# Layer 0 of a four-layer convolution kernel: q (kᵀ v) of two heads as one product with the masked pair, in place of two products on halves of the array

## The chip, the cores and the metric

The kernel runs on one core of one Trainium2 chip. The metric is the device time of the whole program in microseconds (us), the median of three runs. Where a profile is quoted, it is of one execution of the program, with its own time.

## The reference, cut to what matters

x has the shape (T=4, B=8, N=512, D=512). Four layers are added to it one after the other, each on a normalised x. The change lies in layer 0, a spiking attention without softmax; layer 1 is a 13x13 convolution per channel, layers 2 and 3 are 3x3 convolutions over the channels, layer 2 with quantised values.

```python
T, B, N, D, H = (4, 8, 512, 512, 8)
DH = D // H                                   # 64
scale = 1.0 / np.sqrt(D).astype(np.float32)
q = heads(lif(bn(x @ Wq.T, ...)))             # heads: (T, B, H, N, DH), spikes 0 or 1
k = heads(lif(bn(x @ Wk.T, ...)))
v = heads(lif(bn(x @ Wv.T, ...)))
scores = jnp.einsum('tbhnd,tbhmd->tbhnm', q, k) * scale
bias = bias_table[rel].transpose(2, 0, 1)     # depends on m - n and the head alone
scores = scores + bias[None, None]
out = jnp.einsum('tbhnm,tbhmd->tbhnd', scores, v)
out = lif(out.transpose(0, 1, 3, 2, 4).reshape(T, B, N, D))
out = lif(bn((out * gate_scale + gate_shift) @ Wp.T, ...))
```

As there is no softmax, (q kᵀ) v is computed as q (kᵀ v): kᵀ v is only 64x64 for each head. The bias part is a Toeplitz matrix times v, added to it.

## The kernel before

**Steps.** Layer 0 goes through 32 steps (b, t). A step has two halves in the program: `attend` of this step, and then the projections of the next step's input to v, k and q (`project_in`, L499, f32, whole array) with the output projections of this step (`project_out`, L562) between them. So on TensorE's queue a step reads: L515, then L535 with L527 among them, then L499 with L562 among them. The tiles' scheduler sets the order within each engine's queue by priority and readiness as it builds the program[...].

**`attend`, by lines.**

- L515: kᵀ v. The 512 columns of D are four pairs of heads, j = 0 to 3, each 128 columns wide. For each j four products of 128x128 add up a 128x128 block in `ps_kv`: on its diagonal kᵀ v of the two heads, 64x64 each; off the diagonal the products of one head's k with the other head's v, which nobody needs.
- L520: VectorE multiplies all four blocks with a mask of ones in the two diagonal 64x64 squares and zeros elsewhere, and writes them as f16 to `kvb`.
- L527: for each j and each head `two` of the pair, the 128 rows and 64 columns of `kvb` that belong to the head are the stationary operand, and q of the pair (128 rows, 512 columns) streams past. The result lands in 64 partitions of `ps_a`. The first head uses columns 0 to 63 of the array and the second columns 64 to 127 (the trace writes this as 128*64).
- L535: the bias part. For each j 24 products of the same form: 4 blocks of v, 3 bf16 parts of the Toeplitz matrix (`toep`), 2 heads. They add up in `ps_b`, also on 64-column halves.
- L545 (ScalarE, t = 0) or L547 (VectorE) reads `ps_a`; L550 (VectorE) adds `ps_b`; `fire` (L444 and what follows) makes the spikes `so` of this j, which L562 reads.

`ps_a` has one buffer, `ps_b` two, `ps_kv` one. Because `kvb` comes from VectorE, the scheduler puts some L535 between L515 and the first L527 of a step (8, 16 or 9, as it comes), and after that 24 L535 between one pair of L527 and the next.

**After layer 0.** Layer 1 (L815) starts on TensorE when the last step's output projection is done; it uses 112*64 of the array. Layers 2 (L1098, 128*128, bf16) and 3 (L1200, 64*64, f32) run together at the end, a few of one and a few of the other.

Of the kernel before, what the change touches and what calls it, by code (L numbers as in the profile page):

```python
# [45 lines left out]
DH = D // H  # L46
# [220 lines left out]
def layer0(  # L267
    s, tc, i, x_in, x1d, ident, block, avg, group_stats, st1, norm1, band1d, r1, w_sum, shared
):
    nc = tc.nc  # L270
# [171 lines left out]
    def fire(v, h, t, c_col, spikes):  # L442

        nc.vector.tensor_scalar(spikes, v, 1.0, None, op0=ALU.is_ge)  # L444
        if t < T - 1:
            nc.vector.scalar_tensor_tensor(v, v, 1.0, v, op0=ALU.is_lt, op1=ALU.mult)  # L446
            if c_col is None:
                nc.scalar.mul(h, v, 0.5)
            else:
                nc.scalar.activation(h, v, AF.Identity, bias=c_col, scale=0.5)  # L450
# [57 lines left out]
    def attend(got, t):  # L508
        q, k, v = got["q"], got["k"], got["v"]

        kv = ps_1.tile([P, NC, P], F32, tag="misc", name="ps_kv")
        for j in range(NC):
            cut = slice(j * P, (j + 1) * P)
            for c in range(NC):
                nc.tensor.matmul(  # L515
                    kv[:, j, :], lhsT=k[:, c, cut], rhs=v[:, c, cut],
                    start=c == 0, stop=c == NC - 1,
                )
        kvb = work.tile([P, NC, P], F16, tag="kvb", name="kvb")
        nc.vector.tensor_mul(kvb, kv, block.unsqueeze(1).to_broadcast([P, NC, P]))  # L520
        spikes = work.tile([P, NC, N], F32R, tag="so", name="so")
        for j in range(NC):
            pa = ps_1.tile([P, N], F32, tag="pa", name="ps_a")
            pb = ps_b.tile([P, N], F32, tag="pb", name="ps_b")
            for two in range(2):
                out = slice(two * DH, (two + 1) * DH)
                nc.tensor.matmul(  # L527
                    pa[out, :], lhsT=kvb[:, j, out], rhs=q[:, j, :], start=True, stop=True
                )
            for c in range(NC):  # L530
                u = P * (NC - 1 - c)
                for z in range(3):
                    for two in range(2):
                        h = 2 * j + two
                        nc.tensor.matmul(  # L535
                            pb[two * DH : (two + 1) * DH, :],
                            lhsT=v[:, c, h * DH : (h + 1) * DH],
                            rhs=toep[z][:, h, u : u + N],
                            start=c == 0 and z == 0,
                            stop=c == NC - 1 and z == 2,  # L540
                        )
            h = h_of["o"][:, j, :]
            w = work.tile([P, N], F32, tag="v", name="v_o", bufs=3)
            if t == 0:
                nc.scalar.mul(w, pa, half_scale)  # L545
            else:
                nc.vector.scalar_tensor_tensor(  # L547
                    w, pa, half_scale, h, op0=ALU.mult, op1=ALU.add
                )
            nc.vector.scalar_tensor_tensor(w, pb, 0.5, w, op0=ALU.mult, op1=ALU.add)  # L550
            fire(w, h, t, None, spikes[:, j, :])
        return spikes
# [102 lines left out]
    for n in range(-1, last + 1):  # L655
        b, t = steps[max(n, 0)]
        if n >= 0:
            with tc.issue_after(did) if n == 0 else ExitStack():
                so = attend(spikes, t)
            residual = load_x(b, t, "xr")  # L660
            if n == last:
                head = start_layer1()
        if n + 1 <= last:
            spikes = new_spikes()
            g, j = divmod(n + 1, PAIR * T)
# [632 lines left out]
```

## Time and profile before

| | |
|---|---|
| runs | 2936.95, 2939.95, 2939.79 us |
| median of the runs | 2939.79 us |
| the profiled execution | 2938.79 us, span 2937.0 us |
| granted TensorE clock, mean | 0.986 |
| layer 0 on TensorE (first to last of L499 and `attend`) | until about 2050 us |
| layer 1 (L815) | 2050.6 to 2500.9 us |
| layers 2 and 3 (L1098, L1200) | 2513.6 us to the end |
| L535, 3072 matmuls | 368.4 us in which at least one runs, 383 ns each |
| L527, 256 matmuls | 379 ns each (median) |
| L515, 512 matmuls | 219 ns each (median) |

How to read it: [...] the next one starts before it ends. So the time that a matmul takes from the queue is the distance from its start to the start of the next one, called its slot below, and not its duration. The product of the count and the duration says little: 3072 times 383 ns would be three times the 368.4 us in which L535 runs at all. In the listings PE is the matmul, PEld the load of its stationary operand, DVE is VectorE; what stands in brackets is the idle time of the engine before the instruction, and what ended it.

The whole list of costs on the page names L499 first (three rows of some 450 us each), and then L815, L535 and L562; L527 is too small to be among the shown rows.

### The profile page before, as it was taken

How to read it: one execution, taken by the hardware profiler on the slowest of the kernel's cores; microseconds unless marked ns; L12 is line 12 of the kernel's file. 1: busy time of each engine (PE TensorE's matmuls, PEld its weight loads, DVE VectorE, ACT ScalarE, POOL GpSimd, SP SyncE). 2: the span in 40 equal slices, each digit the busy share in tenths (PEclk: the TensorE clock that was granted, in tenths of full speed). 3: DMA queues.
4: the chain of work that ended last, by engine and by line, in shares of the span. 5: the costliest groups of instructions: out<-in, count | busy, mean ns of one | idle time of the engine just before them, and what ended most of it. 6: DMA issues, size and time to landing. Idle time of an engine off the chain costs nothing. (4 is left out here: it accounts for less than half of the span.)

```text
span 2937.0 us, 36614 instructions
## 1 busy us (share of the span) xinstructions
PE 2833.3 (96%) x12865; PEld 1303.7 (44%) x12865; DVE 2214.3 (75%) x3915; ACT 551.2 (19%) x859; POOL 1035.3 (35%) x1928
## 2 busy tenths in 40 slices
PE   6899999999999999999999999999999999589999
PEld 3454555554555545455455555455333333223334
DVE  7897788789779778878877886886655566887870
ACT  1300010011010001001001000110211112766664
POOL 3343234333234323323422433332211112676650
PEclk9899999999999999999999999999999999889999
DMA  7323322222222222222221122113877779698865
GB/s 180 97 81 81 76 58 66 66 73 77 69 61 70 71 75 73 58 66 66 76 68 46 49 54 55 51 42 95 226 194 216 201 208 247 142 204 209 222 171 147
DMA packets 323943, 322.10 MB, mean 110 GB/s; under 512 B 21639, under 2 KB 237391, under 8 KB 323647
## 3 DMA queue, kind: packets, MB, share of 16 engines
q1 hardware_dynamic: 261504, 236.70, 32.9%
q0 software_dynamic: 20192, 56.83, 6.2%
q10 hardware_dynamic: 42063, 26.23, 3.2%
q8 instruction: 101, 1.65, 0.2%
q14 instruction: 83, 0.68, 0.1%
HBM read 210.57 MB, written 103.60 MB: 107 GB/s over the span
## 5 line engine op out<-in xcount | busy, mean ns | idle before, releaser
L499 PE MATMUL ps_in<-w_v,xn 128*128 128x512 f32 x1024 | 459.7, 599 | 3.0 <-DVE xn L480 3.0
L499 PE MATMUL ps_in<-w_kq,xn 128*128 128x512 f32 x1024 | 450.2, 592 | 0.0
L815 PE MATMUL ps_conv<-x,bt 112*64 112x512 f32 x2048 | 445.1, 592 | 0.8 <-DVE v_p L467 0.8
L499 PE MATMUL ps_in<-xn,w_kq 128*128 128x512 f32 x1024 | 444.6, 592 | 0.0
L535 PE MATMUL ps_b<-toep,vtok 128*64 128x512 bf16 x3072 | 368.4, 383 | 1.0 <-DVE v_o L550 1.0
L475 POOL TENSOR_TENSOR h_v<-h_v,c_v 128x512 f32<-128x512 f32 x96 | 121.9, 1270 | 685.1 <-DVE h_v L474 659.4
L450 ACT ACTIVATE h_q<-v_q,c_half 128x512 f32<-128x512 f32 x96 | 69.2, 721 | 1473.0 <-DVE v_q L446 865.1
L584 POOL COPY x1s<-x1s 128x2 f32<-128x2 f32 (+1 forms) x1024 | 227.8, 278 | 272.8 <-DVE x1s L573 272.8
L562 PE MATMUL ps_out<-wp,so 128*128 128x512 f32 x1024 | 308.8, 444 | 0.0
L499 PEld LDWEIGHTS ps_in<-xn,w_kq 128*128 128x128 f32 x1024 | 194.3, 190 | 233.0 <-issue 222.0
L499 PEld LDWEIGHTS ps_in<-w_kq,xn 128*128 128x128 f32 x1024 | 194.2, 190 | 219.9 <-issue 205.0
L499 PEld LDWEIGHTS ps_in<-w_v,xn 128*128 128x128 f32 x1024 | 191.0, 191 | 218.6 <-issue 210.3
L815 PEld LDWEIGHTS ps_conv<-x,bt 112*64 112x64 f32 x2048 | 145.5, 135 | 289.7 <-issue 287.8
L1200 PE MATMUL ps_conv<-x,band_t 64*64 64x512 f32 x2040 | 252.5, 612 | 3.1 <-DVE band_t L1169 3.1
L1065 POOL COPY u<-x 128x512 f32<-128x512 f32 (+1 forms) x172 | 209.3, 1252 | 99.6 <-issue 51.8
L535 PEld LDWEIGHTS <-vtok 128*64 128x64 bf16 x3072 | 175.6, 111 | 154.7 <-issue 5.6
L562 PEld LDWEIGHTS ps_out<-wp,so 128*128 128x128 f32 x1024 | 192.6, 188 | 94.3 <-issue 58.3
L573 DVE SCALAR_TENSOR_TENSOR x1s<-v_p,xr 128x256 f32<-128x256 f32 x256 | 188.6, 776 | 13.9 <-DMA x<-x1s 3.1
L833 POOL DMA_DIRECT2D x<-xo x128 | 71.4, 565 | 313.7 <-ACT xo L822 299.4
L475 POOL TENSOR_TENSOR h_k<-h_k,c_k 128x512 f32<-128x512 f32 x96 | 123.2, 1283 | 135.1 <-DVE h_k L474 135.1
L822 ACT ACTIVATE xo<-ps_conv,off 128x512 f32<-128x512 f32 x128 | 87.9, 687 | 430.9 <-PE ps_conv L815 315.1
L1105 DVE SCALAR_TENSOR_TENSOR x<-ps_conv,inv,u 128x512 f32<-128x512 f32 (+1 forms) x172 | 121.7, 745 | 57.8 <-PE ps_conv L1098 30.6
(190 smaller groups left out, 3279.7 us busy)
## 6 DMA issues: line engine op xcount, KB each, us to landing
x<-x SPq DMA_DIRECT2D x64, 917.0 KB
x<-x SPq DMA_DIRECT2D x168, 256.0 KB
x<-x1s POOLq DMA_DIRECT2D x128, 262.0 KB, 2.6
xq<-in_x SPq DMA_DIRECT2D x128, 256.0 KB
xr<-in_x SPq DMA_DIRECT2D x128, 256.0 KB
out<-o SPq DMA_DIRECT2D x164, 192.0 KB
xs<-in_x SPq DMA_DIRECT2D x112, 256.0 KB
x<-xo ACTq DMA_DIRECT2D x128, 128.0 KB
```

The source lines that it names most:

```text
L475: nc.gpsimd.tensor_add(h, h, c_twice[n])
L499: mm = nc.tensor.matmul(ps, lhsT=lhsT, rhs=rhs, start=k == 0, stop=k == NC - 1)
L535: nc.tensor.matmul(pb[two * DH : (two + 1) * DH, :], lhsT=v[:, c, h * DH : (h + 1) * DH], rhs=toep[z][:, h, u : u + N], start=c == 0 and z ...
L562: nc.tensor.matmul(ps, lhsT=so[:, k, c * P : (c + 1) * P], rhs=wpT[z][:, k, :], start=k == 0 and z == 0, stop=k == NC - 1 and z == 1,)
L573: nc.vector.scalar_tensor_tensor(own, v.rearrange("p (g v) -> p g v", g=PH)[:, two, :], 1.0, by_phase[:, two, :], op0=ALU.is_ge, op1=ALU.add,)
L584: nc.gpsimd.tensor_copy(x1[:, f, u : u + n], x1[:, fm, um - n + 1 : um + 1][:, ::-1])
L815: mm = nc.tensor.matmul(ps[q * M1 : (q + 1) * M1, :], lhsT=bt[:, z, :], rhs=xt[:, w0 : w0 + N_PS1, z : z + NV], start=z == 0, stop=z == SH ...
L822: nc.scalar.activation(xo[:, a, :], ps, AF.Identity, bias=off[:, t : t + 1])
L833: engine.dma_start(bass.AP(dst.tensor, dst.offset + (q * n_half * W1_OUT * B + b) * D + f * NV, [[B * D, W1_OUT], [W1_OUT * B * D, n_half] ...
L1065: nc.gpsimd.tensor_copy(u[:n_p, j, :].rearrange("p (v g) -> p v g", g=PH), x[:, j, :].rearrange("p (g v) -> p v g", g=PH),)
L1105: done["DVE"] = nc.vector.scalar_tensor_tensor(own, ps[:n_p, :], w["inv"][:n_p], u[:n_p, j, :], op0=ALU.mult, op1=ALU.add, accum_out=sums[ ...
L1200: mm = nc.tensor.matmul(ps[j][b * HALF : (b + 1) * HALF, :], lhsT=band[half, b, dx, :], rhs=x3[half, s0 + j, dx : dx + D], start=dx == 0, ...
```

## The change

The inner loop over the two heads of a pair is gone. One matmul has the whole 128x128 block of `kvb` as its stationary operand, and writes all 128 partitions of `ps_a`. As the mask has put zeros into the off-diagonal squares, each head's 64 rows of the result hold the same sums, with zeros added. Nothing else in the program's text changes; the lines below it move up by four, so that L535 becomes L531, and the one product stands at L525.

```diff
         for j in range(NC):
             pa = ps_1.tile([P, N], F32, tag="pa", name="ps_a")
             pb = ps_b.tile([P, N], F32, tag="pb", name="ps_b")
-            for two in range(2):
-                out = slice(two * DH, (two + 1) * DH)
-                nc.tensor.matmul(
-                    pa[out, :], lhsT=kvb[:, j, out], rhs=q[:, j, :], start=True, stop=True
-                )
+            nc.tensor.matmul(pa, lhsT=kvb[:, j, :], rhs=q[:, j, :], start=True, stop=True)
             for c in range(NC):
                 u = P * (NC - 1 - c)
                 for z in range(3):
```

The order of the changed program on TensorE is that of the program before with one load and one product in each place where two and two stood, apart from two L535 that move in the first step and one L499 in three places. On the other engines the order is the same.

## The prediction

> **What bounds the kernel now.** I read the page's busy times, then the sums of the stretch in which the changed code runs, then the instructions in order of time inside one time step, then the weight loads' waits.
>
> ```profile
> PE 2833.3 (96%) x12865; PEld 1303.7 (44%) x12865; DVE 2214.3 (75%) x3915; ACT 551.2 (19%) x859; POOL 1035.3 (35%) x1928
> ```
> ```profile
> 174.00:2042.00 1868.00, 1857.97 (x7614) 939.28 (x7611) 1498.36 (x2496) 138.12 (x209) 632.22 (x1363) 1.00 0.25 65
> ```
>
> The first is the busy time of each engine over the span; the second the sums over 174 to 2042 us, steps 1 to 31 of layer 0: TensorE (first pair of numbers) has an instruction in flight for 1857.97 of 1868.00 us at a granted clock of 1.00, VectorE (third pair) for 1498.36. So in layer 0 TensorE's queue is the clock: a slot added or removed there moves the end, as long as TensorE doesn't then wait for someone. Busy time can't show how full the slots are; the order in time can:
>
> ```profile
> 1038.48 1.45 PE L499 MATMUL ps_in<-xn,w_kq 128*128 128x512 f32 x3
> ...
> 1039.77 1.06 PE L515 MATMUL ps_kv<-vtok,k 128*128 128x128 bf16 x16
> ...
> 1040.76 1.05 PE L535 MATMUL ps_b<-toep,vtok 128*64 128x512 bf16 x8
> 1041.10 0.68 DVE L520 TENSOR_TENSOR kvb<-ps_kv,c 128x512 f16<-128x512 f32 x1
> 1041.84 0.11 PEld L527 LDWEIGHTS <-kvb 128*64 128x64 f16 x2 [0.51 <-DVE kvb L520]
> 1041.84 0.41 PE L527 MATMUL ps_a<-q,kvb 128*64 128x512 f16 x2
> ...
> 1042.08 1.89 PE L535 MATMUL ps_b<-toep,vtok 128*64 128x512 bf16 x16
> ...
> 1043.59 0.11 PEld L527 LDWEIGHTS <-kvb 128*64 128x64 f16 x2
> 1043.81 0.38 PE L527 MATMUL ps_a<-q,kvb 128*64 128x512 f16 x2
> ...
> 1044.02 2.76 PE L535 MATMUL ps_b<-toep,vtok 128*64 128x512 bf16 x24
> ...
> 1049.63 2.76 PE L535 MATMUL ps_b<-toep,vtok 128*64 128x512 bf16 x24
> ...
> 1052.32 1.13 PE L499 MATMUL ps_in<-w_v,xn 128*128 128x512 f32 x2
> ```
>
> The columns are start, length, then engine, line and the part of the array used (rows*columns). Two things matter. First, the two halves already run side by side: the pair of L527 starts at 1043.81 and the next L535 at 1044.02, and 24 L535 take from 1044.02 to 1046.61 (the next L527 in the same listing): 2.59/12 = 0.216 us a pair, for two products of 512 columns. A pair of halves costs what one product costs. Second, a gap appears wherever the array changes between 64-column halves and the whole array. The last of 16 L515 starts at 1039.77+1.06-0.219 (its duration) = 1040.61, its slot of 0.056 ends at 1040.67, yet L535 starts at 1040.76: 0.093 us of nothing. The last pair of L535 starts at 1049.63+2.76-0.38 = 1052.01, its slot ends at 1052.22, L499 starts at 1052.32: 0.096. Between L499 and L515, both on the whole array though of different types, there is none: the third L499 starts at 1039.34 and its slot of 0.429 ends at 1039.77, where L515 starts.
>
> [...] loads of L515 (128 columns) last 98 ns, of L527 (64 columns) 110 ns, so the whole block's load is no dearer than one half's.
>
> **The change part by part.** It removes 128 of 256 matmuls and loads at L527; the lines below move up by four. [...] DVE's multiplication with the block mask (L520) already makes the off-diagonal blocks zero, so no work is added to prepare it.
>
> *The slot itself.* 0.216 for the pair, 0.216 for one product: nothing gained but the 3 ns between the halves' starts.
>
> *The two changes of mode.* The product now stands alone between column-tiled L535, 24 of them on either side. Layer 2 and 3 hold the same figure, a whole-array 16-bit product between tiled ones:
>
> ```profile
> 2699.79 2.81 PE L1200 MATMUL ps_conv<-x,band_t 64*64 64x512 f32 x24
> 2702.53 1.47 PE L1098 MATMUL ps_conv<-xq,band 128*128 128x512 bf16 x6
> 2703.93 2.81 PE L1200 MATMUL ps_conv<-x,band_t 64*64 64x512 f32 x24
> 2706.67 1.47 PE L1098 MATMUL ps_conv<-xq,band 128*128 128x512 bf16 x6
> ```
>
> From 2702.53 to 2703.93 is 1.40 us for six products, where 6 x 0.216 = 1.30: 0.10 more. Single starts in the trace split it: first product to second 227 ns instead of 216 (its load, 95 ns, isn't ahead of it and is only partly covered: +11), the last to the next L1200 308 = 216 + 92. On the way in, the last group of L1200 to L1098 takes 522 instead of a slot of 429: +93. And the first L535 pair after a change takes 240 ns instead of 216 (L515 to L535, all 32 times): +24.
>
> *A visit in the stream* therefore adds: 96 in, 11 for the load, 93 out, 24 for the next pair's load = 224 ns. Steps 1 to 31 have three each (j = 1 to 3), 93 visits: 20.83 us.
>
> *The first visit of a step* (j = 0) waits for kvb anyway: the last pair before it starts at 1041.43 [...]. The way in is hidden behind that wait; without it 96 ns more. The pair after the wait took 240 ns, the product will take 227: -13, and then 93+24: 104 ns. 31 visits: 3.22 us. In the seven steps where half a pair of L535 stands ahead of the product the wait is 326 ns after that half's start, more than 309, so the same holds; an odd half alone ahead of a change takes a slot, but the staggered order ended in such a half before, too: 47 slots both ways.
>
> *The first step* (92 to 124 us) is mixed with other whole-array work. Visits 3 and 4 stand between L499 there, so the change takes two changes of mode away: each now costs 523-429 = 94 on the way in, 24 in the pair, 96 on the way out and about 104 in the next f32 product: 318 ns, twice, -0.64 us. Visits 1 and 2 have whole-array work before and L535 after: one change either way, nothing.
>
> Sum: 20.83 + 3.22 - 0.64 = +23.4 us. No stall goes: kvb is as late as before, and the L547 that reads ps_a gets it one product later as before. Queued behind each delayed product are L535, then L550 on DVE and the next step's L499: all move by the same amount. Nothing covers it, as TensorE is the longest queue. The profiled execution took 2938.79 us (span 2937.0, 1.8 around it): 2962.2. The median of the runs is 1.0 above it: 2963.2.
>
> **The rivals.** *No price for the change of mode (ends not slower).* The gaps of 0.09 could belong to what stands at those places, a semaphore or another bank, and a 128-column product between 64-column ones may slip in. Place: the 124 visits of steps 1 to 31; price 0; the sum would be 128 x 3 ns = -0.4, and -0.6 from step 0 falls away as well: 2939.4. It decides once a visit costs under 5 ns, the pair's own small cost. Against: L515 to L535 share type and operands (vtok) and still show 0.093, all 32 times within 1 ns, in the same place as L1200 to L1098; L499 to L515 shows none.
>
> *Part is absorbed.* Seven steps after the first wait longer for kvb than the usual 0.3 to 0.5 us, up to 2.7:
>
> ```profile
> PE ps_a L527 <- DVE kvb L520: 8.8, 7, 2.3
> ```
>
> DVE is behind there, at 1220 to 1230 without a pause, after a wait for a load of xs. If that load doesn't move along with TensorE, the 0.776 us that a step adds (3 x 0.224 + 0.104) are absorbed in each: 7 x 0.78 = 5.4, giving 2957.8. Against: DVE's work and the buffers of xs follow TensorE's step.
>
> *The load is dearer.* For f32 the first product after a change has 104 ns more. If a 98 ns load of f16 lay bare wholly, 98-11 = 87 more for 93 visits: 8.1 us, 2971.3. L1098's 227 speaks against it.
>
> **How the numbers follow.** Forecast 0.82, part absorbed 0.06, dearer load 0.07, no price 0.05. The unknown costs from both sides: the load between 0 (-11 x 93 = -1.0 us) and bare (+8.1); step 0 between 0 and -0.64; absorption 0 to 5.4. All these end slower. I take 2957 to 2969, which holds the forecast, the absorbed case and most of the way to the dear load. 0.2%, about what a measurement can tell from no change, is 5.9 us; no case but the first rival is inside it, and a little is left for a gain that I don't see: faster 0.01, same 0.04, slower 0.95.
>
> **What would show it.** In the changed kernel's listing: one L525 between L531, with the load no longer ahead of it but at its own start; L531's last start to L525 0.31, L525 to L531 0.32, the first L531 pair 0.24; the period of one j 3.03 us instead of 2.81; a step 0.78 longer, layer 1 starting 23 us later and as long as before. Wrong would be a period of 2.81 (no price), or longer waits at L499 for xn (DVE as the bound).

## The result, and the profile after

The changed kernel takes 2956.01 us in the median of four runs, the kernel before 2938.37 us in the median of its four (the three runs listed above and one of 2936.52): a ratio of 1.007, with a 95% interval of 1.0058 to 1.0082. It is slower, by 17.6 us between the medians. The profiled execution took 2955.41 us, with a span of 2953.6 us.

The busy times of the page, and the sums over 171 to 2042 us, most of steps 1 to 31 of layer 0 (which now end at 2072), show little (the same columns as before):

```profile
PE 2850.1 (96%) x12737; PEld 1292.5 (44%) x12737; DVE 2218.3 (75%) x3915; ACT 550.7 (19%) x859; POOL 1033.6 (35%) x1928
```
```profile
171.00:2042.00 1871.00, 1862.48 (x7355) 919.77 (x7353) 1488.29 (x2479) 138.11 (x209) 631.07 (x1363) 1.00 0.25 64
```

TensorE has 128 matmuls fewer and is busy for 17 us longer: the gaps at a change of mode (about 0.1 us) don't show as idle time, as in the trace the matmul that started 0.31 us earlier lasts 0.38 us and so is still running. Where the time went is seen in the order of time. This is the same step as was shown of the kernel before (start, length, engine, line, operation):

```profile
1052.22 1.05 PE L531 MATMUL ps_b<-toep,vtok 128*64 128x512 bf16 x8
...
1053.30 0.10 PEld L525 LDWEIGHTS <-kvb 128*128 128x128 f16 x1 [0.51 <-DVE kvb L520]
1053.30 0.39 PE L525 MATMUL ps_a<-q,kvb 128*128 128x512 f16 x1
...
1053.62 1.92 PE L531 MATMUL ps_b<-toep,vtok 128*64 128x512 bf16 x16
...
1055.46 0.10 PEld L525 LDWEIGHTS <-kvb 128*128 128x128 f16 x1 [0.41 <-issue]
1055.47 0.39 PE L525 MATMUL ps_a<-q,kvb 128*128 128x512 f16 x1
...
1055.79 2.78 PE L531 MATMUL ps_b<-toep,vtok 128*64 128x512 bf16 x24
...
1058.50 0.39 PE L525 MATMUL ps_a<-q,kvb 128*128 128x512 f16 x1
```

The load of the pair (L527) used to start 0.22 us ahead of its product (1043.59 against 1043.81); now the load at L525 starts at 1055.46 with the product at 1055.47. The 16 L531 before it end their last slot at 1055.37 (1053.62+1.92-0.38 = 1055.16 for the last start, and a slot of 0.21), and the product starts at 1055.47, so no product starts for 0.10 us although the last one's slot is over. From L525 to the next L531 it takes 0.32 us, of which 0.216 is the product's slot. The period of one j is 1058.50-1055.47 = 3.03 us, 2.81 before. The wait for kvb ahead of the first product is 0.51 us as it was.

Cut at the same places of the trace, the two executions compare like this (us; the middle row runs from the first L515 of step 1 to the first matmul of layer 1):

| | before | changed | difference |
|---|---|---|---|
| start and step 0 | 173.40 | 170.48 | -2.9 |
| steps 1 to 31 of layer 0 | 1877.17 | 1901.94 | +24.8 |
| layer 1, until the first matmul of layer 2 | 463.06 | 463.40 | +0.3 |
| layers 2 and 3 | 423.38 | 417.80 | -5.6 |
| span | 2937.0 | 2953.6 | +16.6 |

So layer 0 lost what was expected of it, and 8.5 us came back at both ends, where the change was to take 0.64 us away in the one (step 0) and nothing in the other. The last row is seen in the order of time of layers 2 and 3. First the kernel before, then the changed one, at the same work:

```profile
2672.76 0.57 PE L180 MATMUL gps_x<-gsum_x,avg_same 128*128 128x1 f32 x2 [2.15 <-DVE gsum_x L177]
2673.26 4.25 PE L1200 MATMUL ps_conv<-x,band_t 64*64 64x512 f32 x24
```
```profile
2694.06 0.38 PE L180 MATMUL gps_x<-gsum_x,avg_same 128*128 128x1 f32 x2 [2.15 <-DVE gsum_x L177]
2694.37 2.81 PE L1196 MATMUL ps_conv<-x,band_t 64*64 64x512 f32 x24
```

TensorE waits 2.15 us for VectorE in both. Behind that wait the 24 matmuls of layer 3 take 4.25 us in the one and 2.81 in the other. The granted clock goes with it: over the last 260 us (window; busy times of PE, PEld, DVE, ACT, POOL; granted clock, DMA share, GB/s) it is 0.97 before and 1.00 in the changed kernel.

```profile
2673.60:2937.00 263.40, 253.18 (x1858) 93.36 (x1850) 152.00 (x268) 163.51 (x259) 126.12 (x177) 0.97 0.71 182
```
```profile
2695.80:2953.60 257.80, 246.16 (x1850) 90.93 (x1842) 155.17 (x266) 162.60 (x259) 124.56 (x177) 1.00 0.72 185
```

Two questions were left: a proof of the mechanism in layer 0, and whether these 8.5 us are the change's.

### The profile page after: what moved, and what is told of

Same layout as the page of the kernel before. It is cut to its first block, busy times and chain, and to the rows that moved or that the text cites. A ratio compares the mean times of both kernels' runs of the same rounds, so it can differ in the third digit from the quotient of the medians.

```text
span 2953.6 us, 36334 instructions
## 1 busy us (share of the span) xinstructions
PE 2850.1 (96%) x12737; PEld 1292.5 (44%) x12737; DVE 2218.3 (75%) x3915; ACT 550.7 (19%) x859; POOL 1033.6 (35%) x1928
## 5 line engine op out<-in xcount | busy, mean ns | idle before, releaser
L499 PE MATMUL ps_in<-w_v,xn 128*128 128x512 f32 x1024 | 459.3, 599 | 3.0 <-DVE xn L480 3.0
L499 PE MATMUL ps_in<-w_kq,xn 128*128 128x512 f32 x1024 | 450.2, 592 | 0.0
L499 PE MATMUL ps_in<-xn,w_kq 128*128 128x512 f32 x1024 | 444.6, 592 | 0.0
L531 PE MATMUL ps_b<-toep,vtok 128*64 128x512 bf16 x3072 | 370.8, 386 | 1.1 <-DVE v_o L546 1.1
L499 PEld LDWEIGHTS ps_in<-xn,w_kq 128*128 128x128 f32 x1024 | 194.3, 190 | 233.0 <-issue 222.0
L499 PEld LDWEIGHTS ps_in<-w_kq,xn 128*128 128x128 f32 x1024 | 194.2, 190 | 219.9 <-issue 205.0
L499 PEld LDWEIGHTS ps_in<-w_v,xn 128*128 128x128 f32 x1024 | 191.0, 191 | 218.6 <-issue 210.3
L1196 PE MATMUL ps_conv<-x,band_t 64*64 64x512 f32 x2040 | 245.1, 596 | 3.1 <-DVE band_t L1165 3.1
L531 PEld LDWEIGHTS <-vtok 128*64 128x64 bf16 x3072 | 162.8, 111 | 163.0 <-issue 34.2
L546 DVE SCALAR_TENSOR_TENSOR v_o<-ps_b,v_o 128x512 f32<-128x512 f32 x128 | 88.4, 691 | 114.7 <-PE ps_b L531 114.7
```

Source lines behind the costliest of these rows:

```text
L499: mm = nc.tensor.matmul(ps, lhsT=lhsT, rhs=rhs, start=k == 0, stop=k == NC - 1)
L531: nc.tensor.matmul(pb[two * DH : (two + 1) * DH, :], lhsT=v[:, c, h * DH : (h + 1) * DH], rhs=toep[z][:, h, u : u + N], start=c == 0 and z ...
L1196: mm = nc.tensor.matmul(ps[j][b * HALF : (b + 1) * HALF, :], lhsT=band[half, b, dx, :], rhs=x3[half, s0 + j, dx : dx + D], start=dx == 0, ...
```

## The experiments

Each edit is against the kernel before or the changed kernel, as said. "Start to start" is the distance between the starts of two neighbouring matmuls in the trace.

### The product twice

Against the changed kernel:

```diff
             nc.tensor.matmul(pa, lhsT=kvb[:, j, :], rhs=q[:, j, :], start=True, stop=True)
+            nc.tensor.matmul(pa, lhsT=kvb[:, j, :], rhs=q[:, j, :], start=True, stop=True)
```

> The one product of each pair is issued twice into the same tile (the second writes the same result over the first). Theory: the cost is the two changes of the array's mode around a visit, whatever stands inside. Then the second product adds only its slot: 0.227 between the two (first load bare) and 0.31 out; 124 visits x 0.216 = 27 us over the changed kernel's layer 0, total about 2983. Rival: each whole-array product between column halves is dear by itself (its 128-column load can't be put ahead). Then the second shows 0.31 to 0.32 again and adds 39 us or more, total 2995 and up.

Measured: 2988.36 us (one run). In the order of time on TensorE:

```profile
1065.80 0.39 PE L525 MATMUL ps_a<-q,kvb 128*128 128x512 f16 x1
1066.02 0.38 PE L526 MATMUL ps_a<-q,kvb 128*128 128x512 f16 x1
1066.33 2.78 PE L532 MATMUL ps_b<-toep,vtok 128*64 128x512 bf16 x24
```

The two products stand 0.22 apart (226 ns in the median of 128), the next L532 0.31 behind the second (309), and the way in is the changed kernel's (312). Steps 1 to 31 took 1927.5 us, 25.6 more than the changed kernel's 1901.9, where one slot each was to give 26.8; the shortest step, which is free of waits for VectorE that differ from execution to execution, grew by 0.86 us, four slots of 0.215. (The total is 5 us above the 2983 expected: layers 2 and 3 took 423.4 us here, 417.8 in the changed kernel's profile. More on them below.) A second product in a visit costs its slot and nothing else: the price is that of the visit, not of the product. The rival's 0.31 between the two isn't there.

### Halves on 64 rows and 64 columns

Against the kernel before:

```diff
                 nc.tensor.matmul(
-                    pa[out, :], lhsT=kvb[:, j, out], rhs=q[:, j, :], start=True, stop=True
+                    pa[out, :], lhsT=kvb[out, j, out], rhs=q[out, j, :], start=True, stop=True
                 )
```

> Two products again, but each on 64 rows and 64 columns (rows of its own head only), so that the pair leaves the 128*64 mode without using the whole array. Theory [...]: start to start 0.31 on the way in and out, first L535 pair 0.24, a step of layer 0 about 0.8 us longer than before, total 2955 to 2962. Rival ([...] the 128-column load is the cost): as before, 2938.

Measured: 2962.34 us, just above the 2955 to 2962 expected; ratio 1.0089 (1.0075 to 1.0102).

```profile
1055.82 0.40 PE L527 MATMUL ps_a<-q,kvb 64*64 64x512 f16 x2
1056.16 2.78 PE L535 MATMUL ps_b<-toep,vtok 128*64 128x512 bf16 x24
```

0.34 us from the pair to L535 (3 and 330 ns), where the pair on all rows took 0.22. On the way in 309, and the first L535 pair takes 24 ns more again. No matmul of a visit is on the whole array and no load of it has 128 columns, and yet the cost is the same, some 10 ns a visit more (the shortest step is 62.13 us, 62.09 in the changed kernel, 61.29 before). Leaving the tiling is what costs, in both forms tried. This takes the 128-column load out as a cause of the gaps.

### The pairs behind the bias part of their j

Against the kernel before:

```diff
             pa = ps_1.tile([P, N], F32, tag="pa", name="ps_a")
             pb = ps_b.tile([P, N], F32, tag="pb", name="ps_b")
-            for two in range(2):
-                ...
             for c in range(NC):
                 ...
+            for two in range(2):
+                out = slice(two * DH, (two + 1) * DH)
+                nc.tensor.matmul(
+                    pa[out, :], lhsT=kvb[:, j, out], rhs=q[:, j, :], start=True, stop=True
+                )
             h = h_of["o"][:, j, :]
```

> The kernel before with the pair of L527 put behind the 24 L535 of its j. No change of mode is added. The wait for kvb, 0.3 to 0.5 us a step and up to 2.7 in seven steps, should be covered by 24 L535 instead of 8: theory: 31 steps x 0.3 to 0.4 plus up to 8 us: 2918 to 2930. Rival (the wait is VectorE's and comes back at the next thing TensorE needs from it): 2935 to 2940. It is also the yardstick for the next run.

Measured: 2924.51 us, ratio 0.9958 (0.9945 to 0.9972). Waits of TensorE in steps 1 to 31 (who waited for whom: us in total, times, longest):

```profile
PE ps_a L539 <- DVE kvb L520: 2.5, 2, 1.8
```

It was 8.8 us in 7 waits over the whole program before, and those are only the ones in which no matmul was still running; a normal step's 0.3 to 0.5 us doesn't count there. Steps 1 to 31 fell from 1877.2 to 1866.0 us; the shortest step by 0.20, less than the 0.3 to 0.4 expected, the steps with the long waits by up to 2. About 2 us came back: L180 waited 0.8 us for VectorE, and layer 1 took 464.0 us, 463.1 before. The rest of the wait did not come back.

### One product at the end of the step

All four products stand behind the 96 L535 of a step. The bias part is read first, in place; three of the four tiles come from the banks of the projections, so that no product waits for the one before to be read. Against the changed kernel, shortened:

```diff
-            h = h_of["o"][:, j, :]
-            w = work.tile([P, N], F32, tag="v", name="v_o", bufs=3)
-            ...
+            h = h_of["o"][:, j, :]
+            if t == 0:
+                nc.scalar.mul(h, pb, 0.5)
+            else:
+                nc.vector.scalar_tensor_tensor(h, pb, 0.5, h, op0=ALU.mult, op1=ALU.add)
+        for j in range(NC):
+            if j == 0:
+                pa = ps_1.tile([P, N], F32, tag="pa", name="ps_a")
+            else:
+                pa = ps_mm.tile([P, N], F32, tag="mm", name="ps_a")
+            nc.tensor.matmul(pa, lhsT=kvb[:, j, :], rhs=q[:, j, :], start=True, stop=True)
+            h = h_of["o"][:, j, :]
+            w = work.tile([P, N], F32, tag="v", name="v_o", bufs=3)
+            nc.vector.scalar_tensor_tensor(w, pa, half_scale, h, op0=ALU.mult, op1=ALU.add)
             fire(w, h, t, None, spikes[:, j, :])
```

> The one-product form of the change, but all four products of a step behind its 96 L535, next to the f32 projections that use the whole array as well; the bias part is added first (in place in h_o), the q part after. The change of mode that stood between L535 and L499 is now between L535 and the products, so a step has no more changes than before. Theory: 0.31 in, 0.227, 0.216, 0.216, then L499 without a gap; total within 4 us of the late pairs, 2916 to 2932. Rival (the product itself is dear, 0.2 us each): 25 us more than the late pairs, 2943 to 2955.

Measured: 2922.72 us, ratio 0.9954 (0.9941 to 0.9966).

```profile
1035.63 1.06 PE L515 MATMUL ps_kv<-vtok,k 128*128 128x128 bf16 x16
1036.62 10.55 PE L529 MATMUL ps_b<-toep,vtok 128*64 128x512 bf16 x96
1047.10 1.04 PE L546 MATMUL ps_a<-q,kvb 128*128 128x512 f16 x4
1047.97 1.45 PE L499 MATMUL ps_in<-w_v,xn 128*128 128x512 f32 x3
```

From 1047.10 to 1047.97 four products take 0.87 us, 4 x 0.216 = 0.86, and L499 follows without a gap (216 ns, where L535 to L499 took 309). The same whole-array product that costs 0.23 us more between column halves costs its slot alone here; only the first takes 226 ns. In TensorE's queue two things differ from the changed kernel, the wait for kvb and the changes of mode; the tiles' buffers and the order of VectorE's additions differ too, and the last pair of experiments, in which these are the same, takes them out.

### The changed kernel and the kernel before, more often

No edit.

> The changed kernel once more. Steps 1 to 31 of layer 0 took 1901.9 us in its first profile and 1877.2 before, +24.8, while the total rose by 17.6 only. Theory: the rest (start 2.9 less, layers 2 and 3 5.6 less) belongs to the single execution, as the clock's state falls, and isn't the change's: steps 1 to 31 within 1 us of 1901.9 again, the start 170 to 174, layers 2 and 3 anywhere from 417 to 424, and the total, over more runs, 17 to 25 us above before. Rival (the change speeds up what follows it): start 170.5 and last layers 417.8 again, total 17 above.

> The kernel before once more, for the same question. Theory: steps 1 to 31 within 1 us of 1877.2; start 170 to 174, layers 2 and 3 417 to 424, whichever way they fall. Rival (start and end belong to the kernel): 173.4 and 423.4 again.

Measured: the changed kernel 2955.06 us in five runs, ratio 1.0071 (1.0057 to 1.0085) against 2934.47 us, the median of 25 runs of the kernel before. Steps 1 to 31 missed the 1 us that was expected: 1900.56 against 1901.9, and 1879.65 against 1877.2. In one step of the changed kernel's first execution (at 740.8 us) and one of the kernel before's second (at 1230.7) the clock was at half for 3.4 us. The start moved (173.7 in the changed kernel, 172.2 before), the end did not: 418.42 again in the changed kernel, 423.67 before. By then all four profiles of programs with one product at each place had an end of about 418 us, and all six of programs with two matmuls there one of 422 to 424. So both were profiled twice more:

> The kernel before, third profile. So far layers 2 and 3 took 422 to 424 us in all six profiles of programs with two matmuls at each place of q (k^T v), and 418 in all four with one. Theory (it falls by chance in each execution): 418 in some of the four runs of this call with pairs, or 423 in some with one product. Rival (the count of TensorE's instructions decides[...]): 423 here.

> As the third profile of the kernel before: by chance 418 or 423; by the rival 423.

> The changed kernel, third profile: by chance 418 or 423; by the rival 418 again. Steps 1 to 31 of layer 0 at 1900 to 1902.5 us by either.

> As the third profile of the changed kernel: by chance 418 or 423; by the rival 418.

All eight executions of the two, cut as above:

| | total | start and step 0 | steps 1 to 31 | layer 1 | layers 2 and 3 |
|---|---|---|---|---|---|
| before | 2938.79 | 173.40 | 1877.17 | 463.06 | 423.38 |
| before, 2nd | 2940.57 | 172.19 | 1879.65 | 463.18 | 423.67 |
| before, 3rd | 2939.39 | 173.94 | 1876.96 | 463.06 | 423.56 |
| before, 4th | 2938.74 | 173.31 | 1876.99 | 463.07 | 423.50 |
| changed | 2955.41 | 170.48 | 1901.94 | 463.40 | 417.80 |
| changed, 2nd | 2957.28 | 173.72 | 1900.56 | 462.80 | 418.42 |
| changed, 3rd | 2957.58 | 171.37 | 1902.43 | 463.27 | 418.63 |
| changed, 4th | 2954.79 | 171.69 | 1900.22 | 463.05 | 418.04 |
| difference of the means | +17 | -1.4 | +23.6 | 0.0 | -5.3 |

The theory that the end falls by chance in each execution is wrong for the profiled ones: four to four. The granted clock goes with it: over layers 2 and 3 it is 0.94 to 0.95 in the four of the kernel before and 0.96 to 0.97 in the four of the changed one. The trace holds the stretches of half clock. In the first execution of either kernel each lasts 3.413 us or a multiple of it (but for the last, which outlasts the program), and within one execution all start on one grid of 3.413 us, to 2 ns. Counted from the first matmul of layer 2, and leaving out its first 100 us and the very end, the kernel before has four single ones of 3.4 us, at 159.2, 176.2, 258.2 and 275.2 us. Each is the stretch of the grid that follows a wait of TensorE, 2.15 and 2.19 us at L180 or 1.55 us at L1200. The first of them, with the stretch ahead of it, in which TensorE waits (the columns as above):

```profile
2669.39:2672.81 3.42, 1.27 (x7) 0.42 (x5) 3.35 (x6) 1.13 (x2) 3.19 (x3) 1.00 0.69 155
2672.81:2676.22 3.41, 3.41 (x18) 1.47 (x22) 3.41 (x7) 1.95 (x3) 2.12 (x2) 0.50 1.00 193
```

The changed kernel waits as long at the same places (2.15, 1.55, 2.18 and 1.55 us) and has none there in this execution. What differs is how the waits lie on the grid:

| first execution | first wait, 2.15 us | second, 1.55 us | third, 2.2 us | fourth, 1.55 us |
|---|---|---|---|---|
| before | in one stretch, starts 1.22 us into it: half clock follows | in one, starts 0.84 into it: half | in one, starts 0.96 into it: half | in one, starts 0.63 into it: half |
| changed | cut by a boundary, 1.30 and 0.85: none | in one, starts 1.09 into it: none | cut, 0.48 and 1.70: none | cut, 1.47 and 0.08: none |

The third experiment has as many matmuls as the kernel before, 12865, and so have the pairs at the end of the step (below). Over 2650 to 2700 us, which hold the first two of these places in all three programs, the granted clock is 0.97 in both and 0.93 in the kernel before: one stretch of half clock where that has two (3.4 us at half are 0.034 of 50 us). So the count of instructions alone doesn't decide. What does is not shown: no run moved these waits and nothing else, and the table is read from one trace of each kernel.

Without a profile the end may come out otherwise. The 25 runs of the kernel before fall into 15 from 2931.6 to 2935.3 and 10 from 2937.1 to 2940.5 us; the changed kernel's eleven lie from 2954.4 to 2957.6, but for one at 2961.2. The two groups of the kernel before are as far apart as the two ends, so that its faster runs may well have had the short end; no profile has caught one, and this stays open. What is shown is that the change costs 23.6 us in steps 1 to 31, and that in these eight executions layers 2 and 3 were 5.3 us shorter, at a granted clock of 0.96 to 0.97 instead of 0.94 to 0.95.

### One product behind the bias part, and pairs at the end of the step

The first is the changed kernel with its one product moved as the pairs were in the third experiment; the second is the end-of-step version with this in place of the one product:

```diff
-            nc.tensor.matmul(pa, lhsT=kvb[:, j, :], rhs=q[:, j, :], start=True, stop=True)
+            for two in range(2):
+                out = slice(two * DH, (two + 1) * DH)
+                nc.tensor.matmul(
+                    pa[out, :], lhsT=kvb[:, j, out], rhs=q[:, j, :], start=True, stop=True
+                )
```

> The changed kernel with its one product behind the 24 L535 of its j. Theory: three visits of a step between L535 cost 227 ns each; the fourth stands before L499, which uses the whole array too, and adds no change: 31 steps x (3 x 0.227 - 0.09) = 18 us over the late pairs' steps 1 to 31 (1866.0), so 1884; total about 2942. Rival (each product dear, wherever it stands): 31 x 4 x 0.2 = 25 us, 1891.

> As the run with all four products at the end of a step, but with pairs of halves there. Theory: pair and product both take a slot of 0.216, and the number of changes of mode is the same; pairs pay 0.31 plus 0.10 in the first f32 product at L499, the products 0.31 and 0.01: so the pairs are slower by 31 x 0.09 = 2.9 us in steps 1 to 31, 1871 against 1868.3. Rival (one product is dearer than a pair): 3 us or more faster than 1868.

Measured: one product behind the bias part 2939.33 us (20 runs), ratio 1.0013 (1.0006 to 1.0019); pairs at the end 2922.63 us, ratio 0.996 (0.9946 to 0.9975). The sums over steps 1 to 31 are 1880.6 and 1867.3 us, where 1884 and 1871 were expected; they hold waits for VectorE that differ from execution to execution. The shortest of the steps, from first L515 to first L515, is free of them:

| version | shortest step, us | against the same place with pairs |
|---|---|---|
| before: pair ahead of the bias part | 61.29 | |
| changed: product ahead of it | 62.09 | +0.80 |
| pair behind it | 61.09 | |
| product behind it | 61.67 | +0.58 |
| pairs at the end of the step | 61.09 | |
| products at the end of the step | 61.00 | -0.09 |

0.58 is three visits of 0.224 less 0.09, as expected (3 x 0.227 - 0.09 = 0.59): the fourth product stands next to L499, which uses the whole array too. In the trace of that run:

```profile
1049.04 0.39 PE L537 MATMUL ps_a<-q,kvb 128*128 128x512 f16 x1
1049.36 2.78 PE L530 MATMUL ps_b<-toep,vtok 128*64 128x512 bf16 x24
1052.07 0.39 PE L537 MATMUL ps_a<-q,kvb 128*128 128x512 f16 x1
1052.30 4.03 PE L499 MATMUL ps_in<-w_v,xn 128*128 128x512 f32 x9
```

0.32 us from a product to L530, 0.23 to L499. At the end of the step the product is 0.09 us a step cheaper than the pair, as expected, but the sums don't show it: 1868.25 with products against 1867.29 with pairs, since the products' execution waited 5.5 us for h_o and the pairs' 4.1, and one step with a wait was 2.7 us longer, in which the clock was at half for 3.4 us (at 242.8 us). In the total the two can't be told apart.

## Why the prediction was right

**What bounds the kernel.** Right: in layer 0 the queue of TensorE sets the end; 0.8 us more in most steps (25 of the 30 from step 1 to step 30 grew by 0.78 to 0.88 us in the mean of the four profiles) appeared in the time at which layer 1 starts, and layer 1 was as long as before.

**The slot, and the change of mode.** Right, term by term. On the way in 312 ns were measured where a slot of 213 would have stood, 99 (96 expected); the first product took 11 ns more for its load and 93 ns passed on the way out, 320 in all (320 expected); the first L531 pair took 24 ns more. A visit costs 227 ns, 224 was expected. The traces show these distances, and not what the array does in them. The first visit of a step cost about 0.12 us (0.80 less three visits), as its way in lies behind the wait for kvb: in the kernel before the last pair ahead of it starts at 1041.43, and 0.31 us later, at 1041.74, the load at 1041.84 had not begun. The shortest step grew by 0.80 us (0.776 expected), steps 1 to 31 by 23.6 us between the means of four and four profiles (24.05 expected).

**The first step.** The two visits between whole-array work were to save 0.64 us. In the changed kernel's order of time this stretch reads:

```profile
117.74 1.10 PE L499 MATMUL ps_in<-w_v,xn 128*128 128x512 f32 x2
118.68 0.38 PE L525 MATMUL ps_a<-q,kvb 128*128 128x512 f16 x1
...
119.04 1.10 PE L499 MATMUL ps_in<-w_v,xn 128*128 128x512 f32 x2
119.98 0.38 PE L525 MATMUL ps_a<-q,kvb 128*128 128x512 f16 x1
120.20 1.02 PE L499 MATMUL ps_in<-w_v,xn 128*128 128x512 f32 x2
121.15 1.05 PE L531 MATMUL ps_b<-toep,vtok 128*64 128x512 bf16 x8
```

From the first L499 to L531 it is 121.15-117.74 = 3.41 us. The kernel before took from 120.23 to 124.28 for the same work, 4.05:

```profile
120.23 1.10 PE L499 MATMUL ps_in<-w_v,xn 128*128 128x512 f32 x2
...
124.28 1.05 PE L535 MATMUL ps_b<-toep,vtok 128*64 128x512 bf16 x8
```

The 0.64 us are there, to the digit.

**Absorption.** The rival's 5.4 us didn't come in the sum: steps 1 to 31 differ by 23.6 us in the mean of four against four, where 0.80 in each of the 31 would be 24.8. But the sum hides that the rival was right in some of its steps. Three executions have 3.4 us of half clock in step 10 or 18; with these left out of those two steps, steps 17, 18 and 21 became 0.15 to 0.3 us shorter instead of 0.8 longer. In these the first product of the kernel before stood 1.5 to 2.8 us behind the matmul ahead of it in nearly every execution; in the changed kernel that distance is under 0.9 us in steps 17 and 21 and at most 1.9 in step 18, so the addition was absorbed there. Against 0.80 in each, these three steps saved 3.1 us. Steps 9 and 10 took 1.5 of it back: they grew by 1.6 and 1.5 us, as the same distance rose there. Why the waits moved to earlier steps is open. The forecast's sum holds neither, and that so little of the two is left in 23.6 is luck.

**The total.** 2963.2 us was predicted and 2956.01 measured. That is 1 us below the range's lower end of 2957, which was built on 2939.79 for the kernel before, whose median became 2938.37 with its fourth run; taken as a difference, 17.6 us were measured where 23.4 were forecast and the range means 17.2 to 29.2. So the result lies at the edge of the range, and luck has a part in that: the edge was set for a loss of 5.4 us to absorption in layer 0, and what came was about as much elsewhere. The sum for layer 0 (24.05 for steps 1 to 31) was right to half a microsecond, and the term that was off is one which the sum held at zero: that everything behind layer 0 only moves. It moved, and layers 2 and 3 became 5.3 us shorter by their clock. The start is 1.4 us shorter in the mean instead of 0.64, within what single executions differ by. No view of the kernel before gave the size of the 5.3; but its page showed a granted clock of under 0.9 in two of the last six slices, and this stage did not keep its length when it was shifted: 423.5 us before and 418.2 after, in the means of four.

## What to carry to other kernels

Two products on halves of the columns that stand next to each other cost one slot here, 0.216 us, so nothing was won by joining them; and one product in another tiling than its neighbours cost two changes of mode, with the bare loads behind them some 0.23 us here (99 ns in, 93 out, 11 and 24 in the matmuls behind them), a whole slot more. When matmuls of different tiling are mixed, count the changes in TensorE's order and place the odd ones next to work of their own form: the same four products cost 0.80 us a step between column-tiled ones and less than the pairs next to the f32 projections. And look at what stands behind a wait in the queue: moving the product that waits for VectorE behind work that is ready was worth 0.4% here (2924.51 us with pairs, 2922.72 with products at the end, 2936.34 before), where no form of the product gained anything by itself.

## What the runs showed of the hardware that wasn't expected

- Leaving 128*64 for 64*64 costs as much as leaving it for the whole array: 0.33 us from the 64*64 pair to the next L535, 24 ns in the pair after it. Fewer rows didn't make the change cheaper.
- In the first execution of either kernel all stretches of half clock start on one grid of 3.413 us, to 2 ns. In the kernel before each of four waits of 2.2 and 1.55 us in the last layers lies within one stretch of the grid and was followed by 3.4 us of half clock; in the changed kernel the same waits were followed by none, three of them cut by a boundary and one begun 1.09 us into its stretch. Over the last 260 us the granted clock was 0.97 in two executions before, 1.00 and 0.99 in two of the changed kernel, and layers 2 and 3 were 5.3 us shorter in the means of four, a stage that the change doesn't touch.
